# Two bottleneck blocks on one core: cleared products ahead of the first load, first loads on two queues, one late store on another queue

## The chip, the cores and the metric

The kernel runs on one core of one Trainium2 chip. TensorE (PE in the profile; its weight loads are PEld) multiplies matrices, VectorE (DVE) and ScalarE (ACT) work elementwise, GpSimd (POOL) and SyncE (SP) mostly issue DMAs here. The metric is the device time of one execution in microseconds. Everything is in fp32.

## The reference

x has 16 images of 1024 channels and 32 x 32 pixels. Two residual blocks follow each other. Layer 0 reduces to 256 channels, lets every pixel attend to its 3 x 3 neighbourhood in 32 heads of 8 channels, and goes back to 1024:

```python
h = relu(bn(conv1x1(x, w_conv1), bn1_s, bn1_b))              # 1024 -> 256
q = relu(bn(conv1x1(h, wq))); k = relu(bn(conv1x1(h, wk))); v = bn(conv1x1(h, wv))
kp = unfold3x3(k) + (pos_h + pos_w)                          # 9 taps, zeros outside the image
attn = softmax(einsum('bgdhw,bgdkhw->bgkhw', q, kp), axis=taps)
h = relu(bn(einsum('bgdkhw,bgkhw->bgdhw', unfold3x3(v), attn)))
x = relu(bn(conv1x1(h, w_conv3)) + x)                        # 256 -> 1024
```

Layer 1 is a plain bottleneck; its normalisations use given means and variances:

```python
out = relu(_bn(conv1x1(x, w1)))                              # 1024 -> 256
out = relu(_bn(conv3x3(out, w2, padding=1)))                 # 256 -> 256
x = relu(_bn(conv1x1(out, w3)) + x)                          # 256 -> 1024
```

## The kernel before, in words

**Stages.** The work is a written list of stages. An image passes through conv1 (1024 to 256), qk and v (three 256 to 256 products), the attention on DVE, "fused" (layer 0's last convolution together with layer 1's first, chunk by chunk), "wino" (the 3 x 3 convolution of four images at once as Winograd products of 36 forms), and "u3" (the last sum). Stages of different images are laid side by side so that PE always has products while DVE works on an earlier image's attention. A stage works through chunks of 128 channels; one program product is 128 x 128 weights on 128 x 512 pixels, which the trace shows as two records. conv1 of image 0 has 8 chunks of x (512 KB each) and for each chunk two halves of output channels (n) and two halves of the pixels: 8 records a chunk (`reduce_part`, L390). w1 comes in two pieces of four chunks each: chunks 0 to 3 and chunks 4 to 7 (the "second half" below).

**What lies beside the stages.** The Winograd weights are made on the chip: `winograd_weights` (L276 to L318) reads the 3 x 3 weights in six pieces g0 to g5 of 384 KB (`load_taps`, L273); 14 steps, called f0 to f13 here, form sums on DVE (L286 to L291) and ACT (L284, L285, L292, L294) and store them in DRAM as `uw` (L306, SP's queue). f0 works down the rows of g0, g1 and g2 and stores nothing; each of f1 to f6 goes along one row and stores. The rooms "u" that these steps write belong to the pool `hpool` of five rooms, which also holds h, q, y, a and the scaled weights: whoever takes a room waits until its former content has been used, and a u has been used when its store in DRAM has landed.

**The order.** After each part of a stage the program calls `side.passes()`, which takes one word of the string `ORDER` and does what its letters say: "f" one step of the Winograd weights and, later, of the scaled weights; "j" a step of the attention; "e" its exponentials; "m" a relay load; "a" the attended relu; "w" the relu after a Winograd stage; "." nothing. Every engine takes its instructions in the order of the program, so the words decide which instruction stands before which on ACT, DVE and the queues. Around the start, before's ACT order is: f0 to f3, the two relus of h of image 0 (L1091), f4, f5, the relu of kp (L489), the two relus of q (L489), f6, kp, f7, f8, `by_offset` (L530).

**After conv1.** h is the output of conv1 behind a relu; qk (L476) needs it, then q behind its relu is needed by 16 small products with the position table (L522), whose sums ACT copies as `by_offset` (L530), which frees a bank of PE's accumulators for the next image's conv1. There are four such banks of two halves (`psum`, tag "ps").

**Queues.** SP and ACT issue DMAs on hardware queues, GpSimd on a software queue. At the start, before issues: on SP w1 in three DMAs (chunk 0, chunks 1 to 3, second half; L131), then g0 to g2, wqk, g3 to g5, wv; on ACT x0 in two halves, x1 and the parameters `par`; on GpSimd x2 to x7 (L362), then the table `members` (L188 to L190) and a memset of the room kp, then w3 and u3 to be scaled (L233). The function `at_first` (L1433) writes these first steps down in order; which queue takes a piece is decided in `more_weights` (L115) and `more_loads`.

**The end.** The last four images' last sums are made in pairs of output chunks (`Pair`, L1237 to L1333). The last pair's `result(0)` ends with two relus on ACT and a store of 512 KB on SP (L1329, L1330); `result(1)` of that pair with a DVE operation and a store on SP (L1325); and a split chunk with three stores (L1307 on SP, L1308 on ACT, L1309 on SP).

Of the kernel before, what the change touches and what calls it, by code (L numbers as in the profile page):

```python
# [8 lines left out]
F32 = mybir.dt.float32  # L9
# [4 lines left out]
P = 128  # L14
B, C, H, W = 16, 1024, 32, 32
HW = H * W
# [3 lines left out]
HALF = HW // 2  # L20
# [8 lines left out]
JPIX = JROWS * W  # L29
PW = W + 2  # L30
HALO = (JROWS + 2) * PW
NPOS = 4
# [40 lines left out]
def sa_bottleneck_kernel(ctx: ExitStack, tc: tile.TileContext, x, w1t, wqkvt, w3t, u1t, u2t, u3t, params, out):  # L73
    nc = tc.nc
# [8 lines left out]
    apool = ctx.enter_context(tc.tile_pool(name="apool", bufs=1))  # L83
# [4 lines left out]
    psum = sums_room.enter_context(tc.tile_pool(name="psum", bufs=4, space=bass.MemoryType.PSUM))  # L88
# [12 lines left out]
    def source(name, half):  # L101
# [8 lines left out]
        at = {"wqk": slice(0, 2 * WID), "wv": slice(2 * WID, 3 * WID)}[name]  # L110
        return wqkvt.rearrange("(c p) n -> p c n", p=P)[:, :, at]

    def more_weights():

        if not queue:  # L115
            return
        key = name, of, half = queue.pop(0)
        if spare and name[0] == "U":
            t = lent[key] = spare.pop(0)
        else:  # L120
            t = wpool.tile([P, HW], F32, tag="w", name=f"{name}{half}_{of[0]}")
        src = source(name, half)
        n, k = src.shape[-1], 1
        for d in src.shape[1:-1]:
            k *= d
        view = t[:, : k * n].rearrange("p (c n) -> p c n", n=n)
        if len(src.shape) == 4:
            view = t.rearrange("p (m j o) -> p m j o", m=NW, j=2)
        if of[1] == 0 and name == "w1":
            for part in (slice(0, 1), slice(1, k)) if half == 0 else (slice(0, k),):  # L130
                nc.sync.dma_start(view[:, part], src[:, part])  # L131
        else:
            nc.sync.dma_start(view, src)
        pieces[key] = view
# [52 lines left out]
    def member_table():  # L187
        nc.gpsimd.memset(members, 1.0)  # L188
        for base, sign in ((0, 1), (HEAD_DIM - 1, -1)):
            nc.gpsimd.affine_select(  # L190
                out=members,
                in_=members,
                compare_op=ALU.is_ge,
                fill=0.0,
                base=base,
                pattern=[[-sign * HEAD_DIM, G]],
                channel_multiplier=sign,
            )
# [22 lines left out]
    kp = const.tile([P, NW, H + 2, PW], F32, tag="kp", name="kp")  # L221
# [102 lines left out]
    def halves(half):  # L324
        return slice(half * HALF, (half + 1) * HALF)


    loads, loaded, stored, live = [], {}, {}, [0]

    def more_loads():  # L330

        while loads and live[0] < CHUNKS + RESULTS - 1:
            kind, b, c = loads[0]
            late = kind == "r" and b >= B - NK

            spare = kind == "x" and b < 2 and c >= CHUNKS
            if live[0] >= CHUNKS and not (kind == "x" and b < 2) and not (late and late_rooms):
                return
            if kind == "V":

                if forms.get((b, c[1] == 2), 0) < NK:
                    return
                src = form_room(b)[c[0], c[1]].rearrange("p k j e -> p (k j e)")
            elif kind == "r":
                if (b, c) not in stored:
                    return
                src = stored[b, c]
            else:
                src = x[b, c * P : (c + 1) * P, :]
            name = f"{kind}_{b}_{c}".translate(str.maketrans(" ,", "__", "()"))  # L350
            if late and live[0] >= CHUNKS:
                t = late_of[loads[0]] = late_rooms.pop(0)
                live[0] -= 1
            elif spare:
                t = rpool.tile([P, HW], F32, tag="r", name=name)
            else:
                t = xpool.tile([P, NK * 2 * PART], F32, tag="x", name=name)
                t = t if kind == "V" else t[:, :HW]

            by = nc.scalar if loads[0] in (("x", 0, 0), ("x", 0, 1)) else nc.gpsimd  # L360
            for part in (halves(0), halves(1)) if loads[0] == ("x", 0, 0) else (slice(None),):
                by.dma_start(t[:, part], src[:, part])  # L362
            loaded[loads.pop(0)] = t
            live[0] += 1

# [10 lines left out]
    def free():  # L376

        live[0] -= 1
        more_loads()
# [529 lines left out]
    def finish_winograd(b, n):  # L909
# [4 lines left out]
        )  # L914

    ORDER = (
        ". . f . ff . f ff . . f ff ff . . f . fff fj ffff . jj j j . . . j . jj jj j j jj . . . e j j j j jj "
        "jj . jj j j j . jjjj . . . j j . j . j a j jj . j j j e j . . jj jj . jmjj jj j j . jj . . j . . jj "
        ". . f j f fa . . jf . . . j fjj jj j fj j . . ej jj j jm j fj m . jj . . jj . jjf ffj . . . . . . f "
        "jjfj f fj j . . . jj jj . jjj . . ja . . e j j jjj j m j j . jjj jjj . j . . . j j . f . jfjj . f . "  # L920
        "j . . f jja . fj j . jf j . e jj jfj mjj . . j . jj . m . . jj fj f . . f fff . jjjf . . . . j . . "
        "jj . j . . . . . j . . . . . . . . . . j wjw j jj . j j ejj j j jm . jm j jw j . jw jj . jj . . jj j "
        "j . j j jww . jj j j j jejj ja mjww m j j j . . j j j . j j . jj j . jj . aj jj . . j j j jj . jjej "
        "j m . jjm . . j j jf . a . ff f j . jf . fjf . . . . . jj . jjj j . ff a ff . j f j . fjf . . . . j "
        ". j jjj . f f f f j j ffj . ejj jf m m ff f f . f . j fj jf . j . j . . j j j j j jj . jj . . j . . "
        "jj . j . . j . j . . . . . . . . . . . jw j j je jjjw . mj mj j . j j . j jww . j jjj j . j . jj . j "
        "j . jj jww j j jj ejajj . mj jj w mw . jj . . j j j j jj j . . . j jj . aj . j j j jj . j jje jj j . "
        "jm m j . j j j . . j f f f f j f j . fjjjf . . . j j . j j . f fff . j . fa j . . . j j jj f fjj je "
        "a jjj . . jm . . jj . jjm . j . jjj . j j f . . f f f . j fj . ff . jf . f f . f ffj . jf j . . . . "
        "jj j j j . . . . j . . . . . . . j . . . . . ej j . jmwwjm . jj jj . j wj j jw jj j . j jj . . j j "  # L930
        "wj . jjj a j jw jejj j m . j mj . aj j . . j jj . j j jj j j . . . . j ja . jj . j j jj j j je jjj . "
        "j j . . . j . j jj . . j j jf . f . j ff f . fffffffff af w . w f . . . . . . . . f . . f . ff f . . "
        ". . . ff . f ff f . . . f . . . . . . . . . . . . . . . . . . . ww w www . . w . w . . . . . . . . . "
        ". "
    )

    class Side:
# [85 lines left out]
    for text in (  # L1023
# [5 lines left out]
        for word in text.split():  # L1029
            b, _, of = word[1:].partition(":")  # L1030
# [193 lines left out]
    class Pair:  # L1224
# [86 lines left out]
        def result(self, m):  # L1311
            o = 2 * self.q + m
            t = rpool.tile([P, HW], F32, tag="r", name="result")
            to = out[self.b, o * P : (o + 1) * P, :]
            r_, t_ = self.r[m].rearrange("p (j n) -> p j n", j=4), t.rearrange("p (n j) -> p j n", j=4)
            shift = bn_sh[:, 2 * NW + o : 2 * NW + o + 1]
            if self.end:

                one, two = slice(0, 2), slice(2, 4)
                if m == 1 and not self.last:  # L1320
                    nc.scalar.activation(t_, r_, RELU, bias=shift, scale=1.0)
                    nc.gpsimd.dma_start(to, t)
                elif m == 1:
                    nc.vector.tensor_scalar(t_, r_, shift, 0.0, ALU.add, ALU.max)
                    nc.sync.dma_start(to, t)  # L1325
                else:
                    for i, part in ((2, one), (3, two)):
                        ps = self.banks[i].rearrange("p (j n) -> p j n", j=2)
                        nc.scalar.activation(t_[:, part], ps, RELU, bias=shift, scale=1.0)  # L1329
                    nc.sync.dma_start(to, t)  # L1330
            else:
                nc.scalar.activation(t_, r_, RELU, bias=shift, scale=1.0)
                nc.gpsimd.dma_start(to, t)  # L1333
            free_late(("r", self.b, o))
# [96 lines left out]

    made = []

    def at_first():
        more_weights()
        more_loads()
        nc.scalar.dma_start(par, params)
        more_weights()
        norms()
        load_taps(0)  # L1440
        more_weights()
        load_taps(1)
        more_weights()
        member_table()
        nc.gpsimd.memset(kp, 0.0)
        load_scaled()
        scale_rows()
        position_table()
        side.first(winograd_weights())
        side.first(scale_weights())  # L1450
        hooks["conv1", 2, 0] = clear_hidden
# [44 lines left out]
```

## Time and profile before

The runs of before took 2367.32, 2367.7, 2365.55 and 2366.91 us, median 2367.11. One execution was profiled:

| what | us |
|---|---|
| the profiled execution's own time | 2366.66 |
| its span, first instruction to last event | 2364.9 |
| PE busy (6244 records) | 2348.4 |
| DVE busy | 2163.4 |
| ACT busy | 931.8 |
| GpSimd busy | 490.3 |
| start of the first product | 4.29 |
| first product of qk of image 0 | 34.70 |
| end of the last product | 2358.46 |
| landing of the last store | 2363.97 |

Landings at the start, in us from the span's start: w1 chunk 0 4.05, first half of x0 4.24, its second half 5.80, w1 chunks 1 to 3 6.04, x2 8.56, x1 9.35, x3 10.69, par 11.2, x4 12.42, w1's second half 14.10, x5 14.28, g0 16.35, x6 16.53, g1 18.64, x7 18.81, g2 20.97, w3 21.16 and 23.06, wqk 24.85, u3 25.13 and 27.48.

How the profile is read: times are microseconds from the start of the span. A row of the timeline has start, duration, engine, line, operation, output<-inputs, the shape and a count; brackets give the idle time of the engine before it and what ended it. Busy time of PE counts a product that runs at a low clock as busy, so a low clock is seen in the distance between starts. A queue row (SPq, ACTq) is the issue of a DMA, not its landing. In the table of windows the columns after the window are its length, then the busy time and count of PE, PEld, DVE, ACT and POOL, PE's clock as a share of full speed, the busy share of the DMA engines, and GB/s. A row of DMA issues ends with the KB of one and the median us from issue to landing.

### The profile page before, as it was taken

How to read it: one execution, taken by the hardware profiler on the slowest of the kernel's cores; microseconds unless marked ns; L12 is line 12 of the kernel's file. 1: busy time of each engine (PE TensorE's matmuls, PEld its weight loads, DVE VectorE, ACT ScalarE, POOL GpSimd, SP SyncE). 2: the span in 40 equal slices, each digit the busy share in tenths (PEclk: the TensorE clock that was granted, in tenths of full speed). 3: DMA queues.
4: the chain of work that ended last, by engine and by line, in shares of the span. 5: the costliest groups of instructions: out<-in, count | busy, mean ns of one | idle time of the engine just before them, and what ended most of it. 6: DMA issues, size and time to landing. Idle time of an engine off the chain costs nothing.

```text
span 2364.9 us, 18845 instructions
## 1 busy us (share of the span) xinstructions
PE 2348.4 (99%) x6244; PEld 1142.0 (48%) x6244; DVE 2163.4 (91%) x1786; ACT 931.8 (39%) x890; POOL 490.3 (21%) x900
## 2 busy tenths in 40 slices
PE   9999999999999999999999999999999999999998
PEld 3444444444475444444466444444467444444843
DVE  4899999999989999999989999999989999976687
ACT  3323342324122574443122574324222463444277
POOL 2212121212121332111121232111111231111222
PEclk9999999999999999999999999999999999999999
DMA  9968687878697998687888998688787897699887
GB/s 364 369 217 303 243 287 252 285 273 278 252 351 252 342 390 297 219 265 245 258 313 276 324 387 313 225 274 286 263 294 276 326 374 248 208 355 309 318 294 293
DMA packets 295585, 691.63 MB, mean 292 GB/s; under 512 B 20800, under 2 KB 165184, under 8 KB 286784
## 3 DMA queue, kind: packets, MB, share of 16 engines
q0 software_dynamic: 119888, 471.14, 54.4%
q1 hardware_dynamic: 174944, 218.06, 28.4%
q10 hardware_dynamic: 656, 1.23, 0.2%
q8 instruction: 50, 0.82, 0.1%
q14 instruction: 47, 0.39, 0.0%
HBM read 415.32 MB, written 275.03 MB: 292 GB/s over the span
## 4 chain that ended last, share of the span: by engine, by line
PE 93%; DVE 3%; DMA 3%; ACT 1%; issue 0%; SPq 0%; ACTq 0%; DVEq 0%
PE ps L390 37%; PE ps L422 29%; PE ps L476 13%; PE ps L823 9%; PE ps L1252 4%; DMA a<-a 1%; DVE acc L678 1%; DVE acc L696 1%; DMA U<-uw 1%; DMA uw<-u 1%; PE ps L522 0%; DVE z L849 0%; DVE y L849 0%; ACT kp L489 0%; DVE prod L621 0%
## 5 line engine op out<-in xcount | busy, mean ns | idle before, releaser
L390 PE MATMUL ps<-result,u 128*128 128x512 f32 x1024 | 457.9, 593 | 0.3 <-ACT result L441 0.3
L422 PE MATMUL ps<-a,w 128*128 128x512 f32 x1024 | 457.8, 593 | 0.0
L390 PE MATMUL ps<-x,w 128*128 128x512 f32 x1024 | 445.3, 596 | 4.6 <-DMA x<-in_x_dram 4.3
L678 DVE TENSOR_TENSOR acc<-e,bnv 128x2048 f32<-128x2048 f32 x144 | 327.5, 2283 | 17.1 <-ACT e L660 14.1
L422 PE MATMUL ps<-y,u 128*128 128x512 f32 x768 | 331.1, 593 | 0.0
L621 DVE TENSOR_TENSOR prod<-qc,bnk 128x2048 f32<-128x2048 f32 x144 | 324.1, 2288 | 1.8
L441 ACT ACTIVATE result<-ps,par 128x1024 f32<-128x1024 f32 x128 | 142.4, 1113 | 459.0 <-PE ps L422 379.5
L390 PEld LDWEIGHTS ps<-x,w 128*128 128x128 f32 x1024 | 195.9, 191 | 250.7 <-issue 243.0
L390 PEld LDWEIGHTS ps<-result,u 128*128 128x128 f32 x1024 | 194.8, 190 | 245.2 <-issue 237.4
L422 PEld LDWEIGHTS ps<-a,w 128*128 128x128 f32 x1024 | 195.1, 190 | 244.4 <-issue 243.2
L696 DVE TENSOR_TENSOR acc<-acc 128x2048 f32<-128x2048 f32 x128 | 293.4, 2292 | 4.4
L422 PEld LDWEIGHTS ps<-y,u 128*128 128x128 f32 x768 | 146.2, 190 | 182.9 <-issue 180.7
L476 PE MATMUL ps<-h,wqk 128*128 128x512 f32 x512 | 222.3, 593 | 0.0
L442 POOL DMA_DIRECT2D r<-result x128 | 68.7, 537 | 597.3 <-ACT result L441 593.2
L626 DVE TENSOR_TENSOR prod<-prod 128x2048 f32<-128x2048 f32 (+1 forms) x80 | 166.2, 2077 | 2.3
L476 PEld LDWEIGHTS ps<-h,wqk 128*128 128x128 f32 x512 | 97.4, 190 | 122.3 <-issue 110.8
L441 ACT ACTIVATE result<-ps,bn_sh 128x1024 f32<-128x1024 f32 x96 | 106.7, 1112 | 105.3 <-PE ps L422 103.9
L1091 ACT ACTIVATE h<-ps,par 128x1024 f32<-128x1024 f32 x32 | 38.5, 1204 | 258.3 <-PE ps L390 258.2
L413 ACT ACTIVATE ps<-s 128x1024 f32<-128x1024 f32 x128 | 131.2, 1025 | 14.7 <-DMA s<-in_x_dram 12.3
L489 ACT ACTIVATE kp<-ps,par 128x1024 f32<-128x1024 f32 x64 | 77.2, 1208 | 147.5 <-PE ps L476 118.4
L362 POOL DMA_DIRECT2D x<-in_x_dram x126 | 67.0, 533 | 275.2 <-PE ps L390 206.5
L846 ACT ACTIVATE z<-ps 128x1024 f32<-128x1024 f32 x48 | 49.2, 1024 | 178.8 <-PE ps L823 132.2
(384 smaller groups left out, 2676.0 us busy)
## 6 DMA issues: line engine op xcount, KB each, us to landing
s<-in_x_dram POOLq DMA_DIRECT2D x128, 512.0 KB, 5.8
r<-result POOLq DMA_DIRECT2D x128, 512.0 KB, 4.4
x<-in_x_dram POOLq DMA_DIRECT2D x126, 512.0 KB, 5.3
out_dram<-result POOLq DMA_DIRECT2D x125, 512.0 KB, 6.4
r<-r POOLq DMA_DIRECT2D x111, 512.0 KB, 7.2
v<-v SPq DMA_DIRECT2D x96, 408.0 KB, 4.7
U<-uw SPq DMA_DIRECT2D x60, 512.0 KB, 5.5
bnk<-kp SPq DMA_DIRECT2D x32, 680.0 KB, 6.9
```

The lines of the kernel that those rows point to most:

```text
L390: nc.tensor.matmul(ps[n][:, halves(half)], wt[:, c % (NC // 2), n * P : (n + 1) * P], src[:, halves(half)], start=(c == first), stop=(c == ...
L413: nc.scalar.activation(ps, loaded.pop((self.kind, self.b, o)), AF.Identity)
L422: nc.tensor.matmul(self.ahead[o][:, halves(half)], pieces[key][:, n, o % (NC // 2) * P :][:, :P], self.src[:, n, halves(half)], start=Fals ...
L441: nc.scalar.activation(to_, ps, RELU, bias=self.shift(o), scale=1.0)
L476: nc.tensor.matmul(ps[:, halves(half)], pieces[key][:, m, at : at + P], h[:, m, halves(half)], start=(m == 0), stop=(m == NW - 1),)
L489: nc.scalar.activation(dst, src, func, bias=col(f"L0_conv_{name}_b", n), scale=col(f"L0_conv_{name}_s", n),)
L621: nc.vector.tensor_tensor(by_row(t[:, two]), by_row(qc), kc[:, :, i : i + JROWS, j : j + W], ALU.mult)
L626: nc.vector.tensor_add(u[:, :, 0:4], u[:, :, 0:4], u[:, :, 4:8])
L678: nc.vector.tensor_tensor(by_row(dst), rows(e[:, k, :]).unsqueeze(1).to_broadcast([P, HEAD_DIM, JROWS, W]), vc[:, :, i : i + JROWS, j : j ...
L696: nc.vector.tensor_add(acc, acc, t)
L823: nc.tensor.matmul(acc[i][:, at, :, n, :], pieces[key][:, m, at, n * P : (n + 1) * P], v[:, at, :, m * (TILES + TR) :][:, :, :TILES], star ...
L1252: nc.tensor.matmul(ps, w, by, start=i in (1, 2, 7) and not (i == 2 and self.end), stop=True, skip_group_check=True)
```

## The change

Five things change.

- `warm_up`, called before everything else: DVE clears 128 x 256 of a room of the pool `apool`, and PE makes three products of this cleared data with itself (128 x 128 on 128 x 256) into a bank of the accumulators. Nothing reads the sums; the bank is then used by others.
- The `members` table and the memset of kp are issued before the first loads of x on GpSimd, in place of behind them.
- The first loads: SP takes w1's chunk 0, the second half of x0, x1, x3, then w1's second half and the g pieces; ACT takes the first half of x0, w1's chunks 1 to 3 (`rest`), x2 and par; GpSimd takes x4 to x7 and then w3 and u3.
- The store of the late `result(0)` goes to GpSimd's queue in place of SP's.
- `ORDER` is a new string of as many words (732) with as many of each letter, apart from 12 more dots. On ACT the main difference is at the start: f0 to f2, the two relus of h, f3, f4, kp, the two relus of q, f5, kp, by_offset, f6. On the other engines some neighbours swap places; on SP the loads of `uw` near 1700 us and one near 2085 us move by one or two stores.

Lines behind the new ones have higher numbers: L390 is L398 in the changed kernel, L476 L484, L522 and L530 are 8 higher, L1091 is L1099, L1330 is L1338.

```diff
--- before.py
+++ after.py
@@ -110,6 +110,8 @@
         at = {"wqk": slice(0, 2 * WID), "wv": slice(2 * WID, 3 * WID)}[name]
         return wqkvt.rearrange("(c p) n -> p c n", p=P)[:, :, at]
 
+    rest = []
+
     def more_weights():
 
         if not queue:
@@ -127,8 +129,10 @@
         if len(src.shape) == 4:
             view = t.rearrange("p (m j o) -> p m j o", m=NW, j=2)
         if of[1] == 0 and name == "w1":
-            for part in (slice(0, 1), slice(1, k)) if half == 0 else (slice(0, k),):
-                nc.sync.dma_start(view[:, part], src[:, part])
+            first = 1 if half == 0 else k
+            nc.sync.dma_start(view[:, :first], src[:, :first])
+            if first < k:
+                rest.append((view[:, first:], src[:, first:]))
         else:
             nc.sync.dma_start(view, src)
         pieces[key] = view
@@ -357,9 +361,13 @@
                 t = xpool.tile([P, NK * 2 * PART], F32, tag="x", name=name)
                 t = t if kind == "V" else t[:, :HW]
 
-            by = nc.scalar if loads[0] in (("x", 0, 0), ("x", 0, 1)) else nc.gpsimd
-            for part in (halves(0), halves(1)) if loads[0] == ("x", 0, 0) else (slice(None),):
-                by.dma_start(t[:, part], src[:, part])
+            early = (nc.scalar, nc.sync), (nc.sync,), (nc.scalar,), (nc.sync,)
+            by = early[c] if (kind, b) == ("x", 0) and c < len(early) else (nc.gpsimd,)
+            for at, queue_ in enumerate(by):
+                part = halves(at) if len(by) == 2 else slice(None)
+                queue_.dma_start(t[:, part], src[:, part])
+            if rest:
+                nc.scalar.dma_start(*rest.pop())
             loaded[loads.pop(0)] = t
             live[0] += 1
 
@@ -914,24 +922,24 @@
         )
 
     ORDER = (
-        ". . f . ff . f ff . . f ff ff . . f . fff fj ffff . jj j j . . . j . jj jj j j jj . . . e j j j j jj "
-        "jj . jj j j j . jjjj . . . j j . j . j a j jj . j j j e j . . jj jj . jmjj jj j j . jj . . j . . jj "
...
+        ". f . . . . ff ff . . f . f ffff f f . . . fj . ffff jjffj . . . j . . . jjjj j j . jjj . . e j . jj "
+        "j jj jj . jjj . j j . jjjj . . . j j . j . j a j jj . j j j e j . . jj jj . jmjj jj j j . jj . . j . "
...
     )
 
     class Side:
@@ -1327,7 +1335,7 @@
                     for i, part in ((2, one), (3, two)):
                         ps = self.banks[i].rearrange("p (j n) -> p j n", j=2)
                         nc.scalar.activation(t_[:, part], ps, RELU, bias=shift, scale=1.0)
-                    nc.sync.dma_start(to, t)
+                    nc.gpsimd.dma_start(to, t)
             else:
                 nc.scalar.activation(t_, r_, RELU, bias=shift, scale=1.0)
                 nc.gpsimd.dma_start(to, t)
@@ -1431,7 +1439,18 @@
 
     made = []
 
+    def warm_up():
+
+        t = apool.tile([P, NPOS, JPIX], F32, tag="pc", name="warm").rearrange("p t w -> p (t w)")
+        nc.vector.memset(t[:, : HALF // 2], 0.0)
+        ps = psum.tile([P, HW], F32, tag="ps", name="ps")
+        for _ in range(3):
+            nc.tensor.matmul(ps[:, : HALF // 2], t[:, :P], t[:, : HALF // 2], start=True, stop=True)
+
     def at_first():
+        warm_up()
+        member_table()
+        nc.gpsimd.memset(kp, 0.0)
         more_weights()
         more_loads()
         nc.scalar.dma_start(par, params)
@@ -1441,8 +1460,6 @@
         more_weights()
         load_taps(1)
         more_weights()
-        member_table()
-        nc.gpsimd.memset(kp, 0.0)
         load_scaled()
         scale_rows()
         position_table()
```

## The prediction

> **What bounds the kernel now.** I read the page's busy times first, then PE's waits, then the first 60 us and the last 10 us instruction by instruction, because only there does the change touch the engine that is nearly always busy.
>
> ```profile
> PE 2348.4 (99%) x6244; PEld 1142.0 (48%) x6244; DVE 2163.4 (91%) x1786; ACT 931.8 (39%) x890; POOL 490.3 (21%) x900
> ```
>
> TensorE is busy for 2348.4 of 2364.9 us. What another engine does counts only where PE stands still or after its last product. PE's waits name the places (engine, line, releaser, then total, times, longest):
>
> ```profile
> PE ps L390 <- DMA x<-in_x_dram: 4.3, 1, 4.3
> PE ps L823 <- DMA U<-uw: 1.7, 1, 1.7
> ...
> PE ps L390 <- ACT by_offset L530: 0.3, 1, 0.3
> ```
>
> All idle time is 16.5 us: 4.3 before the first product, about 6.4 after the last one (it ends at 2358.5), some 6 between. The starts of the weight loads show one more loss, which counts as busy:
>
> ```profile
> 5.84 0.65 PEld L390 LDWEIGHTS ps<-x,w 128*128 128x128 f32 x2 [1.05 <-DMA x<-in_x_dram]
> ...
> 9.57 0.34 PEld L390 LDWEIGHTS ps<-x,w 128*128 128x128 f32 x1 [0.52 <-issue]
> 10.23 0.19 PEld L390 LDWEIGHTS ps<-x,w 128*128 128x128 f32 x1 [0.33 <-issue]
> 10.66 0.19 PEld L390 LDWEIGHTS ps<-x,w 128*128 128x128 f32 x1 [0.24 <-issue]
> ```
>
> Products start 0.86 us apart until 9.57 and 0.43 us apart from 10.23: the array ran at half its clock for its first six microseconds. From 4.29 to 10.23 there are seven products, which at 0.43 take 3.0: 2.9 us lost, the change's target. The next views say who uses that gain.
>
> ```profile
> 20.99 0.96 DVE L286 TENSOR_TENSOR g<-g 128x768 f32<-128x768 f32 x1 [6.72 <-DMA g<-in_u2t_dram]
> ```
>
> ```profile
> 32.71 0.40 ACT L294 ACTIVATE u<-g 128x256 f32<-128x256 f32 x1
> 33.18 1.20 ACT L1091 ACTIVATE h<-ps,par 128x1024 f32<-128x1024 f32 x1
> ```
>
> DVE starts the Winograd weights when the last of the first three g arrives (20.97); ACT, in order, finishes its steps of them at 33.11, and only then takes the first relu of h (33.18 to 34.38), though PE had that half sum ready at 33.16. The first q/k product (34.44 for its weights) follows. So PE's sums and ACT's queue meet within 0.1 us: an earlier PE gains nothing unless ACT is earlier too.
>
> **The change, part by part.** *Cleared products.* One memset on DVE, and three products that show as six records of 256 columns at half clock: 0.43 us each (half of 0.86), 2.6 us. The memset has no row; between the nearest ones (0.17 us for 12 columns, 0.96 for 768) I take 0.5. All of it lies in the 4.3 us before x arrives; if it began 1.5 us late it would push the first product by as much. If the clock rises about 5.8 us after the first work, as in before (4.29 to 10.04), then with work from 1.2 on it rises at about 7: half of the 2.9 is left, and up to 2.7 can go. PE's first convolution would end at 32.0 to 33.8 in place of 34.87.
>
> [...]
>
> *First loads.* The first pieces of w1 and x keep their places at the head of SP's and ACT's queues (landed at 4.05 and 4.24), so the first product stays at 4.2 to 4.3. What is moved is the order behind them: on SP the second half of x0, x1 and x3 (1280 KB) now stand before w1's second half, which stands before the g loads; ACT carries w1's other three chunks and x2; GpSimd starts with x4, behind the member table and the memset of kp, which cost x4 a microsecond or two of a 10 us slack. The price is on g:
>
> ```profile
> w<-in_w1t_dram SPq DMA_DIRECT2D x1, 512.0 KB, 12.4
> ```
>
> ```profile
> 3.00:20.00 17.00, 15.71 (x30) 6.86 (x31) 2.39 (x15) 2.65 (x4) 7.52 (x13) 1.00 1.04 399
> ```
>
> The second row is the window 3 to 20 us; its last two figures say that the DMA engines were full and moved 399 GB/s, so order is all that can change. w1's half took 8 us (from 6.04, when the piece before it had landed, to 14.10: 64 KB/us). Behind x3, which I put at 12 to 13, it lands at 18 to 20, about when chunk 4 needs it (4.3 + 4 x 3.43 + up to 1.9 of half clock = 18 to 20). Before g2 lands, SP must bring 3072 KB (128, 256, 512, 512, 512 and three g of 384), ACT 1200 KB, and GpSimd, whose packets are larger, nearly all of its 4096 KB: 8368 KB are 8.57 MB; at 399 GB/s from 3.0 that is 24.5, somewhat less if GpSimd's last pieces are behind. I take 24.3, bounds 23.3 and 25.0, against 20.97. From g2 to the end of ACT's step f2 the trace has 9.5 us (20.99 to 30.47). In the new order f3's four activations stand behind the relus of h, so h's first relu starts at 24.3 + 9.5 = 33.8 (32.8 to 34.5) in place of 33.18, ends 1.2 later, and the first q/k product comes at 35.05 in place of 34.87: **+0.2, bounds -0.8 and +0.9**. PE waits there for about 1 to 2 us and gives back what the clock brought.
>
> *Next gate: q.*
>
> ```profile
> 46.90 2.30 ACT L489 ACTIVATE q<-ps,par 128x1024 f32<-128x1024 f32 x2 [6.15 <-DMA uw<-u]
> ```
>
> ```profile
> 48.52 1.81 PE L522 MATMUL ps<-q,pos 64*32 64x512 f32 x16
> ```
>
> q's room was held by the store of f3's uw (issued 34.70, landed 46.81: 12.1 us, in a full DMA), so ACT was late, and the position products took 1.81 us where a later image's take 1.09. After the change q waits for f2's uw, issued at 24.3 + 11.06 (the distance from g2 in before) = 35.4. The stores of uw near there took 4.9 to 16.5 us; nearest in time is the 12.1: landing 47.5, q done at 49.8, block done 1.07 later (as in before: 49.20 to 50.27) at 50.9: +0.6 in all, **+0.4** beyond the +0.2; bounds 0 and +4.4.
>
> *by_offset before f6.*
>
> ```profile
> 59.42 2.84 PE L390 MATMUL ps<-x,w 128*128 128x512 f32 x6 [0.30 <-ACT by_offset L530]
> ```
>
> by_offset stood behind f6 and f8 on ACT, which waited for uw until 57.71. It now stands behind f5 only, needs the block at 50.9, and PE wants its bank at 59.4. The gap of 0.47 (0.30 by the view) goes: **-0.47, bounds -0.5 and 0**. The other moved words are swaps of neighbours on DVE, ACT and GpSimd, and SP's loads of uw near 1700 and 2085 us have 5 us or more to spare: nothing, and if that cover fails, something like the existing stalls of 0.3 to 0.5 each.
>
> *Late store.*
>
> ```profile
> 2358.09 0.34 SPq L1330 DMA_DIRECT2D out_dram<-result  x1
> 2358.48 0.42 SPq L1325 DMA_DIRECT2D out_dram<-result  x1
> 2359.01 0.72 SPq L1307 DMA_DIRECT2D out_dram<-result  x1
> 2359.85 1.16 SPq L1309 DMA_DIRECT2D out_dram<-result  x1
> ```
>
> SP issues four stores in a row; the fourth, whose data was ready at 2359.16, goes at 2359.85 and lands last (2363.97; the program ends at 2364.9). Without the first, SP is ready at 2359.2: up to 0.7 earlier, and 0.9 if the last issue is shorter too. GpSimd is free (its last issue is at 2354.92 and landed 2.9 later; its stores have a median of 6.4 under load): issued at 2358.1, landed at 2361.0 to 2364.5. The upper end would be last, by 0.5. I take the near row: **-0.7, bounds -0.9 and +0.5**.
>
> [...]
>
> Sum: 0.2 + 0.4 - 0.47 - 0.7 = -0.6. The profiled execution took 2366.66 (span 2364.9 and 1.76 around it), which gives 2366.1; it lies 0.45 below the median of the runs, 2367.11, which gives 2366.5. Forecast: 2366.2.
>
> **Rivals.** *A, the gain is kept* (0.2). g2 lands by 21.8, because its 3 KB packets get more than I allow, or ACT has f2 done before PE needs it. For: f3 no longer stands before h. Against: 1280 KB of x before it on SP. Then the start is worth -1.9 (middle of 1.0 and 2.7): -1.9 - 0.47 - 0.7 = -3.1, time 2363.6.
>
> *B, slower: q's room* (0.2). f2's uw lands late. With 16.5 us it lands at 51.9, q is done at 54.2, the block at 55.3: +5.0 in place of +0.6, sum +3.8, time 2370.5. It decides from a landing 12.7 us after issue, where the sum is zero; halfway, 2368.5. For: the longest rows stand in the same stretch. Against: the stream of loads is done at the same time in both kernels.
>
> *C, GpSimd's store ends last* (0.1): +0.5 in place of -0.7: 2367.3.
>
> *D, the change does not do what it says*: the cleared products don't raise the clock. With ACT as the gate this changes nothing in the main case, so it has no time of its own; it would exclude A.
>
> **How the numbers follow.** Main case 0.5: 2364.4 to 2367.8. A 0.2, B 0.2, C 0.1. The range goes to the far part of A and to B's middle: 2362.8 to 2369.2, and single runs of before alone scatter by 2.1. A measurement here can tell 0.2% (4.7 us) from no change; below 2362.4 lies the edge of A (0.06), above 2371.8 only B with a second stall (0.06); the same: 0.88.
>
> **What would show it.** Right: the first records of PE before 4.3 with no x, starts 0.43 apart by about 7; g2 at 24.3; an idle of 1 to 2 us on PE ahead of the first q/k product at about 35; q's relu at 47 to 48; no wait for by_offset near 59; four late stores, the last SP issue at 2359.2. Wrong: the first q/k product before 33.9 (A), a wait of PE ahead of the position products beyond 2 us (B), a first product after 5.5, or GpSimd's last store landing after SP's (C).

## The result, and the profile after

The changed kernel takes 2370.09 us (median of 38 runs, 2367.53 to 2373.75) against 2365.93 for the kernel before (56 runs beside them): 4.2 us more between the medians (0.18%), ratio of the runs 1.0015 with a 95% interval of 1.0011 to 1.002. It is slower, by less than the 0.2% that I took for the limit of what can be told, and outside my range, which ended at 2369.2. The profiled execution took 2370.25 us (span 2368.5) against 2366.66 (2364.9).

To find the place I matched every product of the changed kernel with the same product of before's profile; the difference of their starts is called the offset below. It changes at few places:

| place in the program | offset, us | what happens |
|---|---|---|
| first product | 0.00 | 4.29 in both |
| seventh record | -1.47 | the clock is up earlier |
| first q/k product | +0.79 | a wait of 2.34 for h |
| last position products | +4.20 | a wait of 2.86 for q |
| the 3.4 us behind them | +5.85 | the clock is at half |
| next image's conv1 | +5.38 | no stall for by_offset |
| first Winograd stage, 680 us | +3.68 | before's wait of 1.73 for U is not there |
| from 2204 us to PE's end | +3.2 to +3.3 | two small steps |

But for the step at 680 us and small ones, all of it lies in the first 60 us. The longest waits of PE after (the view that the prediction shows of before):

```profile
PE ps L530 <- ACT q L497: 2.9, 1, 2.9
PE ps L484 <- ACT h L1099: 2.3, 1, 2.3
PE ps L1260 <- ACT result L449: 1.3, 1, 1.3
PE ps L1448 <- DVE warm L1445: 1.3, 1, 1.3
```

The wait for x at the start is replaced by one for the cleared buffer, and two waits have come: for h and for q. PE's weight loads at the start, after:

```profile
1.25 2.21 PEld L1448 LDWEIGHTS ps<-warm 128*128 128x128 f32 x6 [1.25 <-DVE warm L1445]
4.29 0.50 PEld L398 LDWEIGHTS ps<-x,w 128*128 128x128 f32 x2 [0.82 <-DMA x<-in_x_dram]
...
6.16 0.34 PEld L398 LDWEIGHTS ps<-x,w 128*128 128x128 f32 x1 [0.52 <-issue]
6.81 0.19 PEld L398 LDWEIGHTS ps<-x,w 128*128 128x128 f32 x1 [0.31 <-issue]
```

The six cleared records run from 1.25, and the first record at the full clock starts at 6.81 in place of 10.23. Now DVE's and ACT's rows after, where this gain is spent:

```profile
24.87 0.96 DVE L290 TENSOR_TENSOR g<-g 128x768 f32<-128x768 f32 x1 [9.97 <-DMA g<-in_u2t_dram]
```

```profile
33.94 0.40 ACT L298 ACTIVATE u<-g 128x256 f32<-128x256 f32 x1
34.25 2.28 ACT L1099 ACTIVATE h<-ps,par 128x1024 f32<-128x1024 f32 x2
...
51.09 2.30 ACT L497 ACTIVATE q<-ps,par 128x1024 f32<-128x1024 f32 x2 [3.56 <-DMA uw<-u]
```

g2 lands at 24.78 in place of 20.97. ACT takes h at 34.25, at once behind f2 (one step earlier in the order than before's f3, and still later than before's 33.18). q's relus wait until 51.09 in place of 46.90, for the store of f2's uw. Its row in the DMA issues of 35.5 to 36.5 us, with the KB and the time to landing, then the row of f1's store after (issued at 33.30), then f2's store before (31.5 to 32.5 us):

```profile
x<-in_x_dram POOLq DMA_DIRECT2D x2, 512.0 KB, 14.6
uw<-u SPq DMA_DIRECT2D x1, 768.0 KB, 15.1
```

```profile
uw<-u SPq DMA_DIRECT2D x1, 768.0 KB, 12.4
```

```profile
uw<-u SPq DMA_DIRECT2D x1, 768.0 KB, 4.9
```

The same 768 KB take 4.9 us when they are issued ahead of the next image's eight loads of x, and 15.1 when seven of these are already under way. Ahead of it on SP's own queue stands f1's store, which fell into the same stream: it lands at 45.69, and f2's at 51.01, 5.32 us behind it. PE's rows after, and two windows behind them:

```profile
35.48 14.00 PE L484 MATMUL ps<-h,wqk 128*128 128x512 f32 x32 [2.34 <-ACT h L1099]
52.35 2.21 PE L530 MATMUL ps<-q,pos 64*32 64x512 f32 x16 [2.86 <-ACT q L497]
54.49 7.90 PE L484 MATMUL ps<-h,wv 128*128 128x512 f32 x14
```

```profile
55.00:58.00 3.00, 3.00 (x5) 1.08 (x4) 2.48 (x8) 3.00 (x6) 0.92 (x2) 0.54 1.05 405
58.00:62.00 4.00, 4.00 (x11) 1.84 (x10) 2.15 (x5) 2.15 (x4) 2.50 (x5) 1.00 1.04 387
```

The wait of 2.86 for q is followed by a granted clock of 0.54 in the window 55 to 58 (third figure from the end): the 1.65 us that the offset gains there. At the end, the issues of SP and of GpSimd after:

```profile
2361.38 0.34 SPq L1333 DMA_DIRECT2D out_dram<-result  x1
2361.89 0.34 SPq L1315 DMA_DIRECT2D out_dram<-result  x1
2362.46 0.59 SPq L1317 DMA_DIRECT2D out_dram<-result  x1
```

```profile
2361.58 0.53 POOL L1338 DMA_DIRECT2D out_dram<-result  x1 [2.90 <-ACT result L1337]
```

SP issues its last store 0.77 us after PE's end (2361.69), where before it was 1.39. But the last store lands 5.18 us after its issue in place of 4.13, and the last landing comes 5.95 us behind PE's end in place of 5.51.

### The profile page after: what moved, and what is told of

Its sections match the earlier page's. It is cut to its first block, busy times and chain, and to the rows that moved or that the text cites. A ratio compares the mean times of both kernels' runs of the same rounds, so it can differ in the third digit from the quotient of the medians.

```text
span 2368.5 us, 18862 instructions
## 1 busy us (share of the span) xinstructions
PE 2351.8 (99%) x6250; PEld 1141.2 (48%) x6250; DVE 2163.7 (91%) x1787; ACT 931.3 (39%) x890; POOL 489.8 (21%) x899
## 3 DMA queue, kind: packets, MB, share of 16 engines
q0 software_dynamic: 119744, 470.61, 54.5%
## 4 chain that ended last, share of the span: by engine, by line
PE 92%; DVE 4%; DMA 3%; ACT 1%; issue 0%; SPq 0%; ACTq 0%; DVEq 0%
PE ps L398 36%; PE ps L430 29%; PE ps L484 14%; PE ps L831 9%; PE ps L1260 4%; DMA a<-a 1%; DVE acc L686 1%; DMA g<-in_u2t_dram 1%; DVE acc L704 1%; DMA uw<-u 1%; PE ps L530 1%; DVE z L857 0%; DVE y L857 0%; DMA w<-in_w1t_dram 0%; DVE prod L629 0%
## 5 line engine op out<-in xcount | busy, mean ns | idle before, releaser
L398 PE MATMUL ps<-result,u 128*128 128x512 f32 x1024 | 457.8, 592 | 0.4 <-ACT result L449 0.4
L398 PE MATMUL ps<-x,w 128*128 128x512 f32 x1024 | 443.3, 593 | 0.1
L398 PEld LDWEIGHTS ps<-x,w 128*128 128x128 f32 x1024 | 195.0, 191 | 245.9 <-issue 243.8
L398 PEld LDWEIGHTS ps<-result,u 128*128 128x128 f32 x1024 | 194.4, 190 | 245.7 <-issue 237.9
L484 PE MATMUL ps<-h,wqk 128*128 128x512 f32 x512 | 222.4, 592 | 2.3 <-ACT h L1099 2.3
L484 PEld LDWEIGHTS ps<-h,wqk 128*128 128x128 f32 x512 | 97.1, 190 | 125.2 <-issue 111.2
L1099 ACT ACTIVATE h<-ps,par 128x1024 f32<-128x1024 f32 x32 | 38.4, 1204 | 264.7 <-PE ps L398 264.7
```

Source lines behind the costliest of these rows:

```text
L398: nc.tensor.matmul(ps[n][:, halves(half)], wt[:, c % (NC // 2), n * P : (n + 1) * P], src[:, halves(half)], start=(c == first), stop=(c == ...
L484: nc.tensor.matmul(ps[:, halves(half)], pieces[key][:, m, at : at + P], h[:, m, halves(half)], start=(m == 0), stop=(m == NW - 1),)
```

## The experiments

Theory 1: g2 comes late behind x, so f2 is late; h stands behind f2 (first gate), and f2's store then lies behind the next image's x, and q waits for it (second gate). Theory 2: ACT's new order does it, whatever the loads. Others are named where they belong. Each kernel is compared with the kernel before on its own chip, since that one's median itself lies between 2365.9 and 2369.2 from chip to chip.

**The old loads.** The edit puts the loads, the member table and the memset of kp back:

```diff
-            first = 1 if half == 0 else k
-            nc.sync.dma_start(view[:, :first], src[:, :first])
-            if first < k:
-                rest.append((view[:, first:], src[:, first:]))
+            for part in (slice(0, 1), slice(1, k)) if half == 0 else (slice(0, k),):
+                nc.sync.dma_start(view[:, part], src[:, part])
...
-            early = (nc.scalar, nc.sync), (nc.sync,), (nc.scalar,), (nc.sync,)
...
+            by = nc.scalar if loads[0] in (("x", 0, 0), ("x", 0, 1)) else nc.gpsimd
```

> The changed kernel with the first loads, the member table and the memset of kp in the places they had before; cleared products, new ORDER and the GpSimd store stay. Theory 1 (the store of f2's uw is issued after the next image's x loads and waits behind them, because g2 lands late): g2 is back at about 21.0, f2's uw is issued near 32 and lands by 37 to 38, ahead of the x loads; the first q/k product comes at 33 to 33.7 in place of 35.5, no wait ahead of the position products, offset to before at 60 us -2 to -3.2, time 2 to 4 us below before. Theory 2 (the new order of ACT itself holds q, whatever the loads): the wait of some 3 us ahead of the position products stays and the time is 1 to 4 us above before.

Measured: 2367.53 against 2369.14 of before, ratio 0.9994 (0.9985 to 1.0003), so not to be told from before. f2's uw is issued at 32.15 and lands at 36.85. PE's rows of this kernel:

```profile
33.64 13.90 PE L478 MATMUL ps<-h,wqk 128*128 128x512 f32 x32
47.47 1.09 PE L524 MATMUL ps<-q,pos 64*32 64x512 f32 x16
```

No wait at either gate, the position products take 1.09 us in place of 1.81, and the offset at 60 us is -2.25. With the order and the products of the changed kernel and the old loads, the loss is gone: theory 2 falls. (The loads went back together with the member table and the memset of kp on GpSimd, so these aren't told apart.) The 2 to 4 us that I expected at the end are 1.6; 0.8 are given back at 84 us (below).

**No cleared products.**

```diff
     def at_first():
-        warm_up()
         member_table()
```

> The changed kernel without the three cleared products. Theory 1: ACT is the gate, so the clock rises 2.8 us later, conv1 ends 1.5 us later, PE's wait ahead of the first q/k product shrinks from 2.3 to about 0.9, and the time is that of the changed kernel, 3.5 to 4.5 us above before. Theory 3 (the products themselves cost the time, by the bank that they hold or by the earlier end): back to within 1 us of before.

Measured: 2373.92, 4.8 above before, ratio 1.0024 (1.0015 to 1.0033). The clock is up at 10.58, PE's wait for h is 1.05 in place of 2.34, and the offset at 60 us is +3.99. The products neither cause the loss nor pay: behind ACT's gates their gain is idle time.

**The old order with the new loads.** The edit is the string `ORDER` of before in the changed kernel.

> The changed kernel with the ORDER of before; products, loads and store stay. Theory 1: g2 at 24.8 holds f3 until 24.8 + 12.1 = 36.9 and h behind it; first q/k product at about 38.2; q waits for f3's uw, issued at 38.6 and landed 12 to 15 us later, 50.6 to 53.6; position products done at 54 to 57; time 4 to 8 us above before. Theory 2 (the new order does the harm): within 1.5 us of before.

Measured: 2376.29, 7.2 above before, ratio 1.0028 (1.0017 to 1.0039). PE's rows:

```profile
38.78 15.51 PE L484 MATMUL ps<-h,wqk 128*128 128x512 f32 x32 [5.23 <-ACT h L1099]
55.77 2.18 PE L530 MATMUL ps<-q,pos 64*32 64x512 f32 x16 [1.48 <-ACT q L497]
```

The offset at 60 us is +7.15. The new order is not the harm; it softens what the new loads do.

**The next image's x later.** GpSimd is given 6 us of useless work ahead of the x loads:

```diff
         scale_rows()
+        for _ in range(3):
+            nc.gpsimd.memset(kp, 0.0)
         position_table()
```

> The changed kernel with three more memsets of kp on GpSimd (2.02 us each) behind the scale rows, which hold back the x loads of the next image by 6 us, from 32.4 to about 38.4; nothing else is changed. Theory 1: f1's uw lands by 36 to 39 and f2's, issued at 35.9, by 39 to 42; no wait ahead of the position products and no fall of the clock behind them; offset to before at 60 us about -0.4 in place of +5.4, time 4 to 6 us below the changed kernel, at -2 to +0.5 of before. Theory 2: f2's uw, or ACT's order, holds q as it did; time as the changed kernel or above.

Measured: 2370.97 against 2369.14, ratio 1.0008 (0.9999 to 1.0017). f1's uw lands at 38.19 and f2's at 40.10. The issues of 35.5 to 36.5 us and PE's rows of this kernel:

```profile
uw<-u SPq DMA_DIRECT2D x1, 768.0 KB, 4.4
```

```profile
39.67 11.32 PE L484 MATMUL ps<-h,wqk 128*128 128x512 f32 x26
50.92 1.09 PE L530 MATMUL ps<-q,pos 64*32 64x512 f32 x16
```

f2's store takes 4.4 us in place of 15.1, and the wait for q is gone: the second gate was the store behind the x stream. Work added to an engine took some 2 us off the loss. The time is 1.8 above before where I expected 0.5 at most, and the offset at 60 us +1.21 where I expected -0.4: here the clock fell behind the wait for h (2.5 us), and the records from 35.3 to 39.6 are up to 0.85 apart, which is 1.6 us. In the changed kernel such a fall is covered by the wait for q, as its second profile shows below.

**Before and after once more, on one chip.**

> The kernel before once more, beside the next three, for its waits. In its first profile PE waited 1.7 us for a load of U near 680 us, and the changed kernel's profile has no such wait; the four first experiments have it with 2.1 to 2.8 us, two of them with the clock at half for some 3 us behind it. Theory 1a (that wait varies from run to run and belongs to no part of the change): it is there with 1 to 3 us. Theory 1b (the change takes it away): 1.7 us in before, none in the changed kernel run beside it.

The kernel before, measured: 2370.82 in its single profiled run. PE waits 3.6 us for U at 680, the clock is at half for about 3 us behind it, and the offset to its own first profile is within 0.15 us from 49 us until there (ahead of that up to -0.8, by an earlier clock, given back at the first gate) and +3.1 to +4.2 after. That wait, then, is a matter of the run; before's profile, which I forecast from, had a small one, and the changed kernel's had none.

> The changed kernel once more, beside the next ones. Theory 1: first q/k product 35.0 to 36.0, f2's uw landing 14 to 16 us after its issue, 2.4 to 3.2 us of wait ahead of the position products, offset to before at 60 us +3.7 (clock kept) or +5.4 (clock fallen); time 2 to 5 us above before. Theory 1a: a wait for U near 680 of 1 to 3 us; theory 1b: none.

The changed kernel, measured: 2372.98 against 2368.72, ratio 1.0017 (1.0008 to 1.0025). First q/k product at 35.88, f2's uw 14.89 us from issue to landing, offset at 60 us +3.94; near 685 us a wait of 2.5, this time for a transfer of v. The wait for q was only 1.0, because the clock had fallen behind the one for h and PE came later: the end of the second gate is fixed by the landing, however PE gets there. Theory 1a holds.

**The wait filled.**

```diff
             ps = psum.tile([P, HW], F32, tag="ps", name="ps")
+            if b == 0:
+                for _ in range(3):
+                    nc.tensor.matmul(ps[:, halves(0)], h[:, 0, :P], h[:, 0, halves(0)], start=True, stop=True)
```

> The changed kernel with three more products of h with itself (6 records, 2.6 us) into the bank of the position products, ahead of them, for image 0 alone; the position products then overwrite that bank. Theory 1 (it is the idle time that lets the clock fall to half behind the wait, for 1.65 us): PE idles under 0.6 us there, the records behind the position products are 0.43 apart at once, offset at 60 us +3.7 in place of +5.4; time 0 to 1.7 us below the changed kernel (the less, the more of its executions keep the clock without it). Rival (the clock falls for another reason, such as the small position products): the fall stays, the same time.

Measured: 2373.36 against 2368.72, ratio 1.0019 (1.001 to 1.0028): not to be told from the changed kernel beside it. PE's rows:

```profile
49.37 2.74 PE L523 MATMUL ps<-h 128*128 128x512 f32 x6
52.27 2.18 PE L533 MATMUL ps<-q,pos 64*32 64x512 f32 x16 [0.17 <-ACT q L497]
54.39 7.13 PE L484 MATMUL ps<-h,wv 128*128 128x512 f32 x16
```

The clock stays up behind the wait, and the offset at 60 us is +3.65. But the changed kernel beside it had kept its clock there as well, behind a wait of only 1.0, so this profile can't show that the filling did it; that the fall at this gate differs from run to run, and cost 0 to 1.7 us, is what remains.

**The late store back on SP.**

```diff
-                    nc.gpsimd.dma_start(to, t)
+                    nc.sync.dma_start(to, t)
```

> The changed kernel with the late store back on SP's queue. Theory 1 (the store is no cause of the 4 us; issued from GpSimd it runs beside the last three and lands with them, while from SP it lands 2.6 us after its issue, ahead of them): SP's last issue 0.6 us later, last landing 5.4 to 5.6 us after PE's end in place of 5.9; time 0 to 0.6 us below the changed kernel. Rival (my prediction's term): the last landing 0.4 to 0.7 us later than with GpSimd, time 0.7 us above the changed kernel.

Measured: 2373.09 against 2368.72, ratio 1.0018 (1.0009 to 1.0027); beside it the changed kernel has 1.0017. From PE's end to the last landing it is 5.60 us here and 6.06 there. Over all profiles of this study the mean is 5.70 with the store on GpSimd (eight profiles, 5.44 to 6.06) and 5.59 with it on SP (seven, 5.51 to 5.69): no gain of the move can be told.

**The old loads with the store on SP, with and without the products.** The first is the first experiment's kernel with the store moved back; the second has neither products nor new loads, so it is the kernel before with the new `ORDER` alone.

> The kernel of the first experiment (old loads, cleared products, new ORDER) with the late store on SP as before. Theory 1: offset to before at 60 us about -2.3 again, and the last landing 5.5 to 5.6 us after PE's end in place of 5.8 to 6.0; time 1.4 to 2.8 us below before, the lowest so far. Rival (the start's gain does not reach the end): within 0.6 us of before.

Measured: 2367.54 against 2368.44, ratio 0.9986 (0.9976 to 0.9996); offset at 60 us -2.30. By the medians it is 0.9 us below before, less than I expected; the ratio would make it 0.9 to 5.7, so how much it gains stays open.

> The new ORDER alone on the kernel before (old loads, no cleared products, store on SP). Theory 1 (with g2 at 21 the order is good: h ahead of f3, q's room held by f2's uw, which lands by 37): first q/k product at 34.3 to 34.9, no lost time in the position products (-0.7) and none for by_offset (-0.47), offset at 60 us -0.9 to -1.6; time 0.4 to 1.6 us below before. Rival (the order does harm by itself): above before.

Measured: 2367.15 against 2368.44, ratio 0.999 (0.9982 to 0.9999); offset at 60 us -2.20, more than I expected, because the clock rose at 7.86 without any help. Both are a little below before on their chip (0.9 and 1.3 us by the medians, with intervals that leave out 1), the changed kernel is above it wherever it ran, and the products add nothing that can be told. The next rows say why: the first kernel's PE and ACT at the next image's h.

```profile
84.22 6.28 PE L478 MATMUL ps<-h,wqk 128*128 128x512 f32 x14 [1.19 <-ACT h L1093]
```

```profile
82.97 2.30 ACT L1093 ACTIVATE h<-ps,par 128x1024 f32<-128x1024 f32 x2 [0.86 <-DMA uw<-u]
```

There h's room waits for another uw to land. The second kernel takes its h at 83.00, the first at 82.97; behind it the offsets are -1.02 and -1.05. A third gate stands at 84 us, and what is gained ahead of it beyond 1.0 to 1.5 us (the first experiment keeps 1.48) is lost there.

**The products alone on the kernel before.** The edit is the function `warm_up` and its call.

> The kernel before with the cleared products alone. Theory 1 (in the old order h stands behind f3, whose end at 33.1 is set by g2, so a faster start is given back): conv1 ends 1.5 to 2.5 us earlier, PE then idles as long, first q/k product at 34.4 to 34.9 as before, offset at 60 us between -0.3 and +0.3; time within 0.6 us of before. Rival (the products' gain is kept): offset -1.5 to -2.5 and as much time.

Measured: 2369.88 against 2368.44, ratio 1.0003 (0.9994 to 1.0012): no difference that can be told, though the medians lie 1.4 apart where I expected 0.6 at most. The clock is up at 6.86, conv1 ends 1.0 us sooner (I expected 1.5 at least), and yet:

```profile
33.15 2.28 ACT L1091 ACTIVATE h<-ps,par 128x1024 f32<-128x1024 f32 x2
```

ACT takes h at 33.15, where before it was 33.18; the first q/k product starts at 34.39, and the offset at 60 us is back at about +0.3.

**Both gates opened.** The changed kernel with f2's step behind h (one word of `ORDER`), the 6 us on GpSimd of above, and the store on SP:

```diff
-        ". f . . . . ff ff . . f . f ffff
+        ". f . . . . f fff . . f . f ffff
```

> The changed kernel with its new loads and products, but with f2's step one word later, behind the relus of h; the three memsets of kp on GpSimd that hold back the next image's x by 6 us; and the late store on SP. Theory 1 (two gates, h behind f2 and q behind f2's uw, ate the gain; both are opened here): first q/k product at 32.7 to 33.9 in place of 35.5, f2's uw lands within 6 us of its issue, no wait ahead of the position products, offset at 60 us -1.5 to -2.6; time 0.8 to 2.8 us below before, with g2 still at 24.8. Rival (late g2 costs elsewhere, in the later steps of the weights): offset above -0.5 by 110 us, time at or above before.

Measured: 2373.69 against 2368.44, ratio 1.0022 (1.0013 to 1.0031); the profiled execution took 2378.91, so its rows show more loss than the median has. The first q/k product comes at 33.53 and the offset at 60 us is -2.36, as theory 1 has it; then comes the loss that the rival has, though not by its cause:

```profile
87.75 2.93 PE L484 MATMUL ps<-h,wqk 128*128 128x512 f32 x3 [4.77 <-ACT h L1099]
```

h of the next image starts at 86.49, behind the weights' steps on ACT and a store of uw that holds its room: 4.8 us of waiting on PE and a fall of the clock at the third gate. That store, the ninth of uw, lands at 86.41 here and at 83.27 in the next kernel, which has the late g2 as well but not the 6 us on GpSimd: the 3.1 us between come with these, not with late g2. This time doesn't tell the first two gates apart, so one more kernel has the first one opened alone.

**The first gate alone.** The same word of `ORDER`, nothing else.

> The changed kernel with f2's step one word later, behind the relus of h, and nothing else: the first gate is opened, the second is left. Theory 1 (the cost is set at the second gate, by the landing of f2's uw): first q/k product at 33.0 to 34.0 in place of 35.5 to 35.9, f2's uw issued at 36 to 38 and landed 13 to 16 us later, the wait ahead of the position products grown to 4 to 6 us, offset to before at 60 us still +3.5 to +6.5; time as the changed kernel or up to 1.5 us above, 3.5 to 6 above before. My prediction's picture (the wait for g2 ahead of h is the gate that decides): the 1.5 to 2 us are kept, offset at 60 us +2 to +2.5, time 1.5 to 2 us below the changed kernel.

Measured: 2374.8 against 2369.17, ratio 1.0024 (1.0013 to 1.0034). PE's first q/k product is at 33.10, 2.4 us earlier than in the changed kernel, and the view of its waits has

```profile
PE ps L530 <- ACT q L497: 5.4, 1, 5.4
```

f2's uw lands at 51.02, against 51.01 in the changed kernel, q starts at 51.11 against 51.09, and the offset at 60 us is +5.09. What the first gate gives, the second takes: the loss is set by the landing of f2's uw. And that landing is set by the store ahead of it on SP's queue: f2's uw is issued 1.06 us later here (36.99) and lands at the same time, in both kernels 5.3 us behind f1's (45.70 and 45.69).

But for the kernel with both gates opened, whose loss comes later, the offset at 60 us tells the difference of the medians to within 1.4 us: +5.38 goes with +4.2 (the changed kernel), +3.65 to +4.14 go with +4.3 to +4.8 (the changed kernel again, filled wait, no products, store on SP), +5.09 with +5.6, +7.15 with +7.2, +1.21 with +1.8, +0.3 with +1.4 (products alone), -2.2 to -2.3 with -0.9 to -1.6.

## Why the prediction was wrong

**What held.** The first product stayed at 4.29. The first record at the full clock started at 6.81 (I said about 7). That was luck: I took the 5.8 us from the first work to the rise from one profile, and over the eleven profiles with cleared products this record lies anywhere from 4.80 to 7.14. Conv1's last record started at 32.56 and ended at 33.15, inside 32.0 to 33.8. The gain of "up to 2.7" behind that range, which rival A's -1.9 also uses, no run shows: by the end of conv1 the runs had kept 1.0 us (products alone), 1.7 (the changed kernel) and 2.0 (filled wait). g2 landed at 24.78 (24.3, bounds 23.3 to 25.0). From there to the end of f2 on ACT it was 9.5 us, as read from before. The first q/k product came at 35.48, +0.79 where I took +0.2 with a bound of +0.9; part of this is that my sum set 35.05 against the end of conv1 (34.87) and not against before's first q/k product (34.70), which would have given +0.35, and g2's landing was 0.5 later than the value I took. by_offset's stall of 0.47 is gone. That the products change nothing behind ACT's gate is shown by the kernels without them and with them alone.

**The step that failed** is "Next gate: q". I gave f2's store the 12.1 us of f3's in before, "nearest in time", and with it +0.4. It took 15.07 us, was issued at 35.93 (I said 35.4), landed at 51.01, and the position products ended 4.2 us later than before. The row was chosen by its time since the start. It prices the first store that falls into the stream of x loads: before, f1's and f2's had gone out ahead of the stream, and f3's was that first store. After, it is f1's (issued at 33.30, behind two loads of x), and it took 12.39, as the row says. But f2's is then the second, behind f1's on SP's queue, and that the step left out. In all seven profiles in which f1's store is still under way when f2's goes out, f2's lands 5.3 to 5.6 us behind it, whenever it was issued (35.93 to 36.99). The loads ahead are not the whole of it: with the new order and the old loads f3's store goes out behind seven loads but with no store under way on SP's queue, and takes 10.2 to 10.7 (three profiles). The fitting rows were f4's and f5's in before, each behind another store in the same stream, with 13.6 and 16.5; both lie beyond the 12.7 from which I had rival B decide. Against rival B I had argued that "the stream of loads is done at the same time in both kernels". The start of the next stream is not: GpSimd's queue had fewer loads ahead of the copies that its instructions wait for (the first copy landed at 25.50, before at 27.75), so the x loads began 1.75 us sooner while the stores of f1 and f2 were issued 3.9 us later. B's sign, a wait beyond 2 us ahead of the position products, came with 2.86. Its chance of 0.2 was too low; its price stands: from the landing, 51.01 + 2.30 + 1.07 gives 54.4 for the end of the position products, measured 54.5.

**A term that I didn't have**: the clock falls again behind a wait. In the profile after it cost 1.65 us at q. No sum of mine has it, for the pauses of 1 to 2 us that I expected or for longer ones. At the gates the clock fell behind waits of 5.37 us (q, the first gate alone), 5.23 (h, the old order), 4.77 (the next image's h, both gates opened), 2.86 (q, the changed kernel), 2.7 (h, its second profile) and 2.48 (h, the next image's x later), and not behind 2.70 (h, the filled wait), 2.36 (q, no products) and 2.34 (h, the changed kernel).

**The late store.** The term -0.7 was wrong. The issue came 0.6 us earlier after PE's end, as I said, but I counted the landing behind an issue as fixed. The store from GpSimd took 5.44 us to land where I took 2.9, and the last one 5.18 in place of 4.13; with the store back on SP they are 2.63 and 4.19. Why the two took longer in the changed kernel no run shows. The means over all profiles say 0.1 us for the worse, inside this step's bounds of -0.9 and +0.5 and far from the value I took.

**A term that the profile of before made too small.** PE's wait for U at 680 us, 1.7 there, none in the profile after, is 2.1 to 3.6 us in all thirteen others (in two of them for a transfer of v), with and without the change, and with a fall of the clock at times. It explains why the two first profiles differ by 3.6 and not by 5.4, and it is no effect of the change.

The sum by the measured terms, as seen in the two first profiles: +0.8 to h, +3.4 to q, +1.65 of clock, -0.5 for by_offset, -1.7 at 680 us, -0.4 for small steps, +0.4 at the end: +3.6.

## What to carry to other kernels

Follow a gain past the first engine that has to take it up: here a faster start of TensorE (conv1 1.0 us sooner with the products alone) was worth nothing by 60 us (offset +0.3), because ACT took h at 33.15 (before at 33.18), and what the first gate gave (2.4 us in the kernel with it alone) the store that held the next room took; three such gates stand in 84 us. Size the landing of a store by what stands ahead of it, the unfinished stores of its own queue above all and the streams of the others, not by the row that is nearest in time (here 4.9 us ahead of the stream, 15.1 within it and behind another store), and ask of every change of load order which later stream it lets start sooner (here by 1.75 us). A wait on TensorE cost more than its length here where the clock fell behind it: 1.3 us more behind the 5.37 for q (the first gate alone), 1.5 behind the 5.23 for h (the old order), 1.65 behind the 2.86 for q (the changed kernel).

## What the runs showed of the hardware

The time of the clock's rise varies without any change of the work: in the four profiles without cleared products the first full-rate record is at 7.86 (the new `ORDER` alone), 7.91 and 10.23 (before, twice) and 10.58 us (no products), with them (eleven profiles) at 4.80 to 7.14. In ten of these eleven TensorE then stood still for 0.1 to 1.2 us between 7 and 10 us, in most by its waits for x, so that an early clock was not all gain even ahead of the gates.

The fall behind a wait did not go by its length alone: 2.7 us for h cost 1.5 us of clock in the changed kernel's second profile and 2.48 for h cost 1.6 in the kernel with the next image's x later, while 2.70 for h in the kernel with the filled wait cost none (the 32 records behind it took 14.00 us, as behind the 2.34 of the changed kernel's first profile). In that first profile the granted clock was 0.50 from 54.38 to 57.79 us, 3.41 us long, behind the 2.86 for q, and 1.00 from there to 62. What decides beside the length was not shown.

A store of 768 KB (uw) needed between 4.2 and 5.6 us ahead of the stream of eight loads of 512 KB, 8.4 to 12.4 as the first store within it, and 13.5 to 17.3 behind another store there with six loads or more under way: the place of an issue, in its own queue and in the streams of the others, was worth some ten microseconds.
